# Preactivation convolution: half sums multiplied an image ahead and written by the vector engine to where the convolution accumulates; three of eight images combined

## The chip, the cores and the metric

The kernel runs on one core of a Trainium2 chip. The metric is the device time of one launch in microseconds (us), the median of several runs. The core has five engines that run their own instruction queues in order: TensorE (PE, with its weight loads shown as PEld), VectorE (DVE), ScalarE (ACT), GpSimd (POOL) and SyncE (SP). They wait for one another by semaphores. Matmuls accumulate in PSUM; everything else lies in SBUF.

## The reference

160 images of 128 channels and 32x32 pixels. Each is group-normalised (32 groups of 4 channels), convolved 3x3 with padding 1 by one of five weight sets (image i of the input uses set i mod 5), and added to the unnormalised input. The weights are quantised from U with two step sizes taken from the range of all of U.

```python
s1 = (beta - alpha) / 3.0                       # beta, alpha: max and min of U
v1 = s1 * floor(U / s1)
s2 = s1 / 5.0
v2 = s2 * floor((U - v1) / s2)
w = (v1 + v2).reshape(OUT_CH * N, IN_CH, K, K)
...
xb = x.reshape(B // N, N * C, H, W)
act = conv_general_dilated(xb, w, window_strides=(1, 1), padding=[(1, 1), (1, 1)], feature_group_count=N)
...
m = jnp.mean(g, axis=(2, 3, 4), keepdims=True)  # g: (B, 32, 4, 32, 32)
s = jnp.var(g, axis=(2, 3, 4), keepdims=True)
gn = ((g - m) / jnp.sqrt(s + eps)).reshape(v.shape)
...
x = x + conv(gn(x), U)
```

## The kernel before, in words

The kernel takes the images set by set: image i of the program (0 to 159) belongs to set i // 32. In SBUF an image is a tile of 128 partitions (channels) by 1024 pixels. A matmul takes one 128x128 weight tap and up to 512 pixels, so an image's output, called eo, fills two PSUM banks of 16 rows each.

The normalised image is used as a sum of two fp16 parts, high and low. For an ordinary image the high part is convolved directly (`taps`, L590): three columns of taps, each 3 rows of taps by 2 banks, 18 matmuls. The low part is convolved through pairs of rows: with d (differences of rows two apart) and s, t (sum and difference of the two rows of a pair), the tap rows g0, g1, g2 give an even and an odd output row as d times g0 or -g2, plus half of (m1 + m2) or (m1 - m2), where m1 = s times (g0 + g1 + g2) and m2 = t times (g0 - g1 + g2). So there are 6 wide matmuls for m1, m2 (PSUM tile m, two banks) and 12 of half width for d. A combined image (`combined`, L504; before: every third one from image 14 to 155) treats both parts this way: 12 wide and 24 half-width matmuls, and no direct taps. `combine` (L514) forms d, s and t in fp32 from the raw image, `high_combined` (ACT) rounds it to fp16, `low_combined` (DVE) takes the rest.

The loop of `run` (from L845) has one iteration for each image. The order of every engine's queue is written out by hand: what `run` calls first comes first on that engine. In iteration i of the kernel before:

- PE: `conv(i)`: m1 and m2 of image i (first, or after the first column of taps if image i-1 is combined), and its taps or products into eo. Two small statistics matmuls (`means`, `variances`) come between columns, once for each group of eight images.
- ACT: for image i+14 the two passes of the statistics (`image_sum` L193, `image_square` L200), `leave(i)` (L674), which copies m1 and m2 from PSUM to SBUF, then `normalise` and `high_part` (L493, L501) of image i+3, or `high_combined` (L537) of image i+2.
- DVE: `low_combined` (L543) or `low_part` (L550), `residual(i-1)` (L707, L709: eo plus the half sums into an fp32 tile sum), `combinations` (L563 to L566), one or two of the 14 steps for a column of the next set's weights (`make_column`), and `pairs(i)` (L686, L687), which forms m1 + m2 and m1 - m2 in SBUF.
- POOL: `accumulate` (L722) issues a DMA that adds sum to the image in SBUF; the small vectors of the statistics (L220 to L245) and two edge rows of `combine` (L522, L523) are computed here.
- SP: issues loads 20 images ahead and stores two images behind.

[...]eo has two buffers of two banks (pool `ps_eo`), m one buffer of two banks (`ps_m`), the statistics one bank and the weight transposes one. Images 0 to 2 are convolved directly in both parts, and the last four are added and stored by hand (`by_hand`). Statistics of images 8, 10, 12 and 14 are made on DVE by bn_stats (L183), all others from image 8 on by ACT.

## Time and profile before

| What | us |
|---|---|
| median of the runs | 1043.59 (1042.65 to 1043.96) |
| the profiled execution, its own time | 1041.9 |
| its span in the profile | 1040.1 |
| PE busy | 995.6 |
| DVE busy | 937.8 |
| ACT busy | 848.7 |
| POOL busy | 436.4 |

The span is the time from the first to the last instruction that the profiler recorded; the execution's own time lies 1.8 us above it. Busy time is the sum of the stretches in which the engine had an instruction. A line number such as L709 is a line of the kernel; a group of instructions shows its count, its busy time, the mean duration of one, and what ended the engine's idle time ahead of it. DVE and ACT start an instruction slightly before the recorded end of the one ahead, so an instruction takes up less of its queue than its recorded duration. The granted TensorE clock was 0.993 of full speed as a mean.

### The profile page before, as it was taken

How to read it: one execution, taken by the hardware profiler on the slowest of the kernel's cores; microseconds unless marked ns; L12 is line 12 of the kernel's file. 1: busy time of each engine (PE TensorE's matmuls, PEld its weight loads, DVE VectorE, ACT ScalarE, POOL GpSimd, SP SyncE). 2: the span in 40 equal slices, each digit the busy share in tenths (PEclk: the TensorE clock that was granted, in tenths of full speed). 3: DMA queues.
4: the chain of work that ended last, by engine and by line, in shares of the span. 5: the costliest groups of instructions: out<-in, count | busy, mean ns of one | idle time of the engine just before them, and what ended most of it. 6: DMA issues, size and time to landing. Idle time of an engine off the chain costs nothing. (4 is left out here: it accounts for less than half of the span.)

```text
span 1040.1 us, 15860 instructions
## 1 busy us (share of the span) xinstructions
PE 995.6 (96%) x5910; PEld 578.5 (56%) x5910; DVE 937.8 (90%) x1374; ACT 848.7 (82%) x1133; POOL 436.4 (42%) x494
## 2 busy tenths in 40 slices
PE   1899998999999999999999999999989999999997
PEld 0455565565655556565555555655545556555553
DVE  8998798998999999889999989998979898888885
ACT  4899796998888888888888889888869988886551
POOL 4432435361454566253545362634554523334210
PEclk9999999999999999999999999999989999999999
DMA  9559988899999889999999999999988999988673
GB/s 370 211 152 233 252 236 229 215 269 273 284 271 255 240 237 264 265 281 256 253 252 268 250 255 258 276 273 266 225 236 222 271 284 241 264 205 220 163 182 125
DMA packets 67286, 254.42 MB, mean 245 GB/s; under 512 B 5248, under 2 KB 5248, under 8 KB 67200
## 3 DMA queue, kind: packets, MB, share of 16 engines
q1 hardware_dynamic: 45168, 173.09, 48.6%
q0 software_dynamic: 22032, 80.23, 40.3%
q8 instruction: 48, 0.79, 0.3%
q14 instruction: 38, 0.31, 0.1%
HBM read 89.19 MB, written 83.89 MB: 166 GB/s over the span
## 5 line engine op out<-in xcount | busy, mean ns | idle before, releaser
L590 PE MATMUL eo<-hi,wt 128*128 128x496 f16 (+3 forms) x1998 | 481.4, 378 | 2.5 <-DVE sum L709 1.2
L626 PEld LDWEIGHTS <-wt 128*128 128x128 f16 x3690 | 361.7, 98 | 217.5 <-issue 2.4
L722 POOL DMA_DIRECT2D xt<-sum x153 | 135.6, 888 | 488.0 <-DVE sum L709 319.1
L590 PEld LDWEIGHTS <-wt 128*128 128x128 f16 x2070 | 203.7, 100 | 196.4 <-issue 6.5
L626 PE MATMUL eo<-rows,wt 128*128 128x248 f16 (+1 forms) x1308 | 197.4, 274 | 0.0
L200 ACT ACTIVATE junk<-xt,mv 128x1024 f16<-128x1024 f32 x156 | 178.6, 1145 | 1.7
L193 ACT ACTIVATE junk<-xt 128x1024 f16<-128x1024 f32 x156 | 164.4, 1054 | 11.7 <-DMA xt<-in_x_dram 10.1
L626 PE MATMUL m<-rows,wt 128*128 128x496 f16 (+1 forms) x654 | 159.2, 380 | 0.0
L674 ACT ACTIVATE mm<-m 128x1024 f16<-128x1024 f32 x109 | 111.0, 1018 | 58.2 <-PE m L626 55.9
L543 DVE SCALAR_TENSOR_TENSOR vl<-v,rstd,vh 128x2048 f16<-128x2048 f32 x48 | 112.7, 2347 | 45.7 <-ACT vh L537 45.7
L493 ACT ACTIVATE z<-xt,shift,rstd 128x1024 f32<-128x1024 f32 x112 | 138.0, 1232 | 6.1 <-POOL shift L243 6.1
L550 DVE TENSOR_TENSOR lo<-z,hi 128x1024 f16<-128x1024 f32 x112 | 137.1, 1224 | 6.4 <-ACT hi L501 6.4
L709 DVE SCALAR_TENSOR_TENSOR sum<-pq,eo 128x1024 f32<-128x1024 f16 x105 | 127.1, 1210 | 3.4 <-PE eo L626 3.4
L501 ACT CAST hi<-z 128x1024 f16<-128x1024 f32 x112 | 116.1, 1036 | 0.4
L537 ACT ACTIVATE vh<-v,rstd 128x2048 f16<-128x2048 f32 x48 | 95.8, 1997 | 23.5 <-POOL v L523 23.0
L626 PE MATMUL eo<-vl,wt 128*128 128x248 f16 (+1 forms) x576 | 110.1, 273 | 0.0
L626 PE MATMUL eo<-vh,wt 128*128 128x248 f16 (+1 forms) x576 | 110.1, 273 | 0.0
L626 PE MATMUL m<-vh,wt 128*128 128x496 f16 (+1 forms) x288 | 110.1, 382 | 0.0
L626 PE MATMUL m<-vl,wt 128*128 128x496 f16 (+1 forms) x288 | 109.9, 382 | 0.0
L674 ACT ACTIVATE mw<-m 128x1024 f32<-128x1024 f32 x48 | 49.1, 1023 | 60.5 <-PE m L626 60.3
L522 POOL TENSOR_SCALAR v<-xt,ngm 128x32 f32<-128x32 f32 x48 | 90.6, 1888 | 0.0
L563 DVE TENSOR_TENSOR rows<-lo 128x1024 f16<-128x1024 f16 x109 | 74.2, 681 | 0.1
(113 smaller groups left out, 971.0 us busy)
## 6 DMA issues: line engine op xcount, KB each, us to landing
xt<-in_x_dram SPq DMA_DIRECT2D x78, 1024.0 KB, 9.2
out_dram<-xt SPq DMA_DIRECT2D x78, 1024.0 KB, 5.3
xt<-sum POOLq DMA_DIRECT2D x153, 512.0 KB, 6.8
range<-in_L_conv_U_dram SPq DMA_DIRECT2D x4, 576.0 KB, 6.4
u<-in_L_conv_U_dram SPq DMA_DIRECT2D x4, 576.0 KB, 12.0
xt<-in_x_dram SPq DMA_DIRECT2D x4, 512.0 KB, 9.4
out_dram<-xt SPq DMA_DIRECT2D x3, 512.0 KB, 2.8
u<-in_L_conv_U_dram SPq DMA_DIRECT2D x2, 288.0 KB, 3.0
```

Source lines behind the costliest of these rows:

```text
L193: self.nc.scalar.activation(junk, image, ACTF.Copy, scale=-1.0 / image.shape[1], accum_out=self.mv[:, j, 0:1],)
L200: self.nc.scalar.activation(junk, image, ACTF.Square, bias=self.mv[:, j, 0:1], accum_out=self.mv[:, j, 1:2],)
L493: nc.scalar.activation(z, self.image(i), ACTF.Identity, bias=st.shift[:, j : j + 1], scale=st.rstd[:, j : j + 1],)
L501: self.nc.scalar.copy(hi.rearrange("p h w -> p (h w)"), self.z[i])
L537: self.nc.scalar.mul(vh, self.v[i], st.rstd[:, j])
L543: self.nc.vector.scalar_tensor_tensor(vl, self.v[i], st.rstd[:, j], self.hi[i], ALU.mult, ALU.subtract)
L550: self.nc.vector.tensor_sub(lo[:, 1 : self.H + 1, :].rearrange("p h w -> p (h w)"), self.z.pop(i), self.hi[i].rearrange("p h w -> p (h w)"),)
L590: nc.tensor.matmul(target[:, h, r0 - h0 : r1 - h0, c0:c1], self.wts[n, col][:, k, :], tile[:, s0 : s0 + r1 - r0, c0 + dw : c1 + dw], start ...
L626: nc.tensor.matmul(target[:, :, c0:c1], self.wts[n, col][:, kind, :], source[:, :, c0 + dw : c1 + dw], start=start, stop=stop,)
L674: self.nc.scalar.mul(m, self.m.pop(i).rearrange("p a i w -> p a (i w)"), scale)
L709: nc.vector.scalar_tensor_tensor(self.sum[i], self.m.pop(i), 0.5 / UP, eo, ALU.mult, ALU.add)
L722: self.nc.gpsimd.dma_start(self.image(i), self.sum.pop(i), accum_op=ALU.add)
```

## The change

The multiplications that form m1 and m2 move an image ahead: iteration i now begins on PE with `sums_of_pairs(i + 1)`, ahead of the taps of image i. ACT copies only m2 to SBUF (`leave(i + 1)`, 512 elements in place of 1024). DVE adds and subtracts m1, read from PSUM, and m2, and writes the two results straight into the PSUM banks of eo of image i+1 (`pairs(i + 1)`). The matmuls of that image then accumulate on what lies there: no matmul of an image from 3 on has `start=True` in eo. Since eo then holds twice the result, the direct taps and the taps for d are kept doubled, and the factor 0.5 is applied as the result leaves PSUM: `residual` becomes one ScalarE instruction (for the last four images it stays on DVE). The fp16 copies of the half sums and their scale UP go.

Combined images are now those with i mod 8 in (1, 4, 6), 53 of them in place of 48. Statistics of images with i mod 8 in (1, 5), from image 9 on, are made by DVE. The order within an iteration is rewritten, `combine` comes two iterations earlier, the buffers of vh go from one to two and those of sum from three to four, and the transposes of a weight column go into the next iteration.

The diff, without blank lines and cut to its core:

```diff
     STEADY = 14
+    COMBINED = (1, 4, 6)
+    MEASURED = (1, 5)
     EARLY = 8
...
         self.wide = pool("wide", 1)
-        self.wide_parts = pool("wide_parts", 1)
+        self.wide_parts = pool("wide_parts", 2)
         self.evac = pool("evac", 2)
-        self.sums = pool("sums", 3)
+        self.sums = pool("sums", 4)
...
+            self.keep_column(n, col, self.turn_column(n, col, parts))
         else:
             m = self.qpool.tile([P, P, ROW], MM, tag="m", name=f"m{n}_{col}")
-            yield nc.vector.scalar_tensor_tensor(m, k1, 5.0, k2, ALU.mult, ALU.add)
-            parts = ((m, self.ident),)
+            nc.vector.scalar_tensor_tensor(m, k1, 5.0, k2, ALU.mult, ALU.add)
+            self.columns.append((n, col, ((m, self.ident),)))
+            yield
...
+        return pt
+    def keep_column(self, n, col, pt):
+        nc, P = self.nc, self.P
         wt = self.wpool.tile([P, 6, P], MM, tag=f"wt{col}", name=f"wt{n}_{col}")
-        nc.scalar.mul(wt[:, self.G, :], pt, 1.0 / LIFT)
-        nc.scalar.mul(wt[:, self.MINUS_G2, :], pt[:, 2, :], -1.0 / LIFT)
+        half = self.qpool.tile([P, ROW, P], MM, tag="half", name=f"half{n}_{col}")
         outer = self.qpool.tile([P, P], MM, tag="outer", name=f"outer{n}_{col}")
-        nc.gpsimd.tensor_tensor(outer, wt[:, 0, :], wt[:, 2, :], ALU.add)
-        nc.gpsimd.tensor_tensor(wt[:, self.SUM, :], outer, wt[:, 1, :], ALU.add)
-        nc.gpsimd.tensor_tensor(wt[:, self.DIFF, :], outer, wt[:, 1, :], ALU.subtract)
+        nc.scalar.mul(wt[:, self.G, :], pt, 2.0 / LIFT)
+        nc.scalar.mul(half, pt, 1.0 / LIFT)
+        nc.gpsimd.tensor_tensor(outer, half[:, 0, :], half[:, 2, :], ALU.add)
+        nc.gpsimd.tensor_tensor(wt[:, self.SUM, :], outer, half[:, 1, :], ALU.add)
+        nc.gpsimd.tensor_tensor(wt[:, self.DIFF, :], outer, half[:, 1, :], ALU.subtract)
+        nc.gpsimd.tensor_scalar_mul(wt[:, self.MINUS_G2, :], wt[:, 2, :], -1.0)
         self.wts[n, col] = wt
...
     def by_vector(self, i):
-        return self.EARLY <= i < self.EARLY + 8 and i % 2 == 0
+        return i >= self.EARLY and i % 8 in self.MEASURED
     def measure(self, i, stages=(0, 1)):
@@ -503,7 +521,7 @@
     def combined(self, i):
-        return self.STEADY <= i < self.imgs - LAST and i % 3 == 2
+        return self.STEADY <= i < self.imgs - LAST and i % 8 in self.COMBINED
     def column_of(self, i):
...
                     tile[:, s0 : s0 + r1 - r0, c0 + dw : c1 + dw],
-                    start=(col == self.COLS[0] and k == 1 and top == 0),
+                    start=(i < self.FIRST and col == self.COLS[0] and k == 1 and top == 0),
                     stop=(last and k == 2),
+                    skip_group_check=True,
                 )
...
+    def product(self, target, i, kind, source, col, start, stop):
+        n, _ = self.place(i)
+        dw = col - 1
+        c0, c1 = max(0, -dw), self.W - max(0, dw)
+        self.nc.tensor.matmul(
+            target[:, :, c0:c1],
+            self.wts[n, col][:, kind, :],
+            source[:, :, c0 + dw : c1 + dw],
+            start=start,
+            stop=stop,
+            skip_group_check=True,
+        )
...
+    def both(self, i):
+        return [self.halves(v) for v in ([self.hi[i]] if self.combined(i) else []) + [self.v[i]]]
+    def sums_of_pairs(self, i):
+        m = self.m[i] = self.banks(self.ps_m, "m", i)
+        both = self.both(i)
+        for a, kind in enumerate((self.SUM, self.DIFF)):
+            for col in self.COLS:
+                for j, (_, st) in enumerate(both):
+                    self.product(
+                        m[:, a], i, kind, st[:, a], col,
+                        col == self.COLS[0] and j == 0,
+                        col == self.COLS[-1] and j == len(both) - 1,
+                    )
     def conv(self, i, on_the_way):
-        nc, W = self.nc, self.W
-        n, _ = self.place(i)
-        combined = self.combined(i)
-        if combined:
-            both = [self.halves(v) for v in (self.hi[i], self.v.pop(i))]
-        else:
-            both = [self.v.pop(i)]
-        late = self.combined(i - 1)
...
-        if not late:
-            sums_of_pairs()
-        eo = self.eo[i] = self.banks(self.ps_eo, "eo", i)
+        if i + 1 < self.imgs:
+            self.sums_of_pairs(i + 1)
+        eo = self.eo[i]
         for col in self.COLS:
-            if col == self.COLS[1] and late:
-                sums_of_pairs()
             if col != self.COLS[0]:
                 on_the_way(col)
-            if not combined:
+            last = col == self.COLS[-1]
+            if not self.combined(i):
                 self.taps(i, (self.hi[i], 0), col, eo, False)
             for a, kind in enumerate((0, self.MINUS_G2)):
-                for d, _ in both:
+                both = self.both(i)
+                for j, (d, _) in enumerate(both):
                     for h in range(2):
                         rows = slice(h * 16 + a, h * 16 + 16, 2)
-                        to = eo[:, h].rearrange("p (i a) w -> p i a w", a=2)[:, :, a, :]
-                        product(
-                            to, kind, d[:, rows, :], col,
-                            combined and col == self.COLS[0] and a == 0 and d is both[0][0],
-                            col == self.COLS[-1] and a == 1 and d is both[-1][0],
+                        to = eo[:, h].rearrange("p (i a) w -> p a i w", a=2)[:, a]
+                        self.product(
+                            to, i, kind, d[:, rows, :], col, False,
+                            last and a == 1 and j == len(both) - 1,
                         )
+        del self.v[i]
     def leave(self, i):
...
-        if self.combined(i):
-            m = self.wide.tile([self.P, 2, 512], F32, tag="m", name=f"mw{i}")
-            scale = 0.5
-        else:
-            m = self.evac.tile([self.P, 2, 512], MM, tag="mm", name=f"mm{i}")
-            scale = UP
-        self.nc.scalar.mul(m, self.m.pop(i).rearrange("p a i w -> p a (i w)"), scale)
-        self.m[i] = m
+        m2 = self.evac.tile([self.P, self.H // 2, self.W], F32, tag="m2", name=f"m2_{i}")
+        self.nc.scalar.copy(m2, self.m[i][:, 1])
+        self.m[i] = self.m[i], m2
...
     def pairs(self, i):
         nc = self.nc
-        m = self.m.pop(i).rearrange("p a (i w) -> p a i w", w=self.W)
-        if self.combined(i):
-            pq = self.wide.tile([self.P, 1024], F32, tag="pq", name=f"pqw{i}")
-        else:
-            pq = self.evac.tile([self.P, 1024], MM, tag="pq", name=f"pq{i}")
-        rows = pq.rearrange("p (i a w) -> p i a w", a=2, w=self.W)
-        nc.vector.tensor_add(rows[:, :, 0], m[:, 0], m[:, 1])
-        nc.vector.tensor_sub(rows[:, :, 1], m[:, 0], m[:, 1])
-        self.m[i] = pq
-        if self.by_hand(i):
-            xj = self.image(i)
-            nc.vector.scalar_tensor_tensor(xj, pq, 0.5 / UP, xj, ALU.mult, ALU.add)
+        m, m2 = self.m.pop(i)
+        eo = self.eo[i] = self.banks(self.ps_eo, "eo", i)
+        rows = eo.rearrange("p h (i a) w -> p (h i) a w", a=2)
+        nc.vector.tensor_add(rows[:, :, 0], m[:, 0], m2)
+        nc.vector.tensor_sub(rows[:, :, 1], m[:, 0], m2)
...
         if not self.by_hand(i):
             self.sum[i] = self.sums.tile([self.P, 1024], F32, tag="sum", name=f"sum{i}")
-            if self.combined(i):
-                nc.vector.tensor_add(self.sum[i], eo, self.m.pop(i))
-                return
-            nc.vector.scalar_tensor_tensor(
-                self.sum[i], self.m.pop(i), 0.5 / UP, eo, ALU.mult, ALU.add
-            )
+            nc.scalar.mul(self.sum[i], eo, 0.5)
             return
         xj = self.image(i)
         halves = [slice(0, 512), slice(512, 1024)] if i == self.imgs - 1 else [slice(0, 1024)]
         for h in halves:
-            nc.vector.tensor_add(xj[:, h], eo[:, h], xj[:, h])
+            nc.vector.scalar_tensor_tensor(
+                xj[:, h], eo[:, h], 0.5, xj[:, h], ALU.mult, ALU.add
+            )
...
-        ready, middle, measured, loaded, later = [], [], self.EARLY, 6, None
+        ready, middle, measured, loaded = [], [], self.EARLY, 6
+        later, turned = iter(()), []
...
                     for st in ready:
                         st.means()
+                    for *column, parts in self.columns:
+                        turned.append((column, self.turn_column(*column, parts)))
+                    self.columns.clear()
...
             if i < self.FIRST:
+                if i == self.FIRST - 1:
+                    self.sums_of_pairs(self.FIRST)
                 j = (i - 1) % self.FIRST
                 self.direct_hi(j, self.COLS[2])
@@ -863,79 +871,70 @@
...
-                self.residual(j)
                 for col in self.COLS:
                     on_the_way(col)
             else:
+                j = i - 1
                 self.conv(i, on_the_way)
             ahead = i + min(10 + i // 2, self.STAT_LEAD + 1)
             to_measure = range(measured, min(self.imgs, ahead))
             measured += len(to_measure)
...
-            parted = [
-                k for k in (i + 3, i + 4)
-                if self.FIRST < k < self.imgs and not self.combined(k)
-                and k - 3 - (self.combined(k - 1) and self.group_of[k] == self.group_of[k - 1])
-                == i
-            ]
-            if b == self.per_set // 16 and n + 1 < N_SETS:
-                self.load_set(n + 1)
-            if b == self.per_set // 8 and n + 1 < N_SETS:
-                later = (s for col in self.COLS for s in self.make_column(n + 1, col))
+            if n + 1 < N_SETS:
+                if b == (2 if n == 0 else 0):
+                    self.load_set(n + 1)
+                if b == (4 if n == 0 else 2):
+                    later = (s for col in self.COLS for s in self.make_column(n + 1, col))
             by_scalar = [k for k in to_measure if not self.by_vector(k)]
...
+            if i != self.FIRST:
+                self.residual(j)
+                self.accumulate(j)
+            if self.combined(i + 1):
+                for k in by_scalar:
+                    self.measure(k, (0,))
+            if self.FIRST <= i + 1 < self.imgs:
+                self.leave(i + 1)
+            if not self.combined(i + 1):
+                for k in by_scalar:
+                    self.measure(k, (0,))
+            part = self.FIRST < i + 3 < self.imgs
+            if self.combined(i + 3):
+                self.high_combined(i + 3)
+            elif part:
+                self.normalise(i + 3)
             for k in by_scalar:
-                self.measure(k, (0,))
-            if self.combined(i - 1):
-                for k in by_scalar:
-                    self.measure(k, (1,))
-            if i >= self.FIRST and not self.combined(i):
-                self.leave(i)
-            for k in parted:
-                self.normalise(k)
-            if self.combined(i):
-                self.leave(i)
-            elif not self.combined(i - 1):
-                for k in by_scalar:
-                    self.measure(k, (1,))
-            for k in parted:
-                self.high_part(k)
-            low = i + 2 if self.FIRST < i + 2 < self.imgs and not self.combined(i + 2) else None
-            if self.combined(i + 1):
-                self.low_combined(i + 1)
-            if self.combined(i + 2):
-                self.combine(i + 2)
-                self.high_combined(i + 2)
-            if low is not None:
-                self.low_part(low)
-            if i > self.FIRST:
-                self.residual(i - 1)
-                self.accumulate(i - 1)
-            if low is not None:
-                self.combinations(low)
-            if later is not None:
-                take(later, 1)
-            if i >= self.FIRST:
-                self.pairs(i)
-            if later is not None:
-                take(later, 1)
-                if b == self.per_set - 1:
-                    run(later)
+                self.measure(k, (1,))
+            if part and not self.combined(i + 3):
+                self.high_part(i + 3)
             for st in middle:
                 st.deviation()
                 st.scales()
             for st in ready:
                 st.deviations()
+            for column, pt in turned:
+                self.keep_column(*column, pt)
+            turned = []
+            low = i + 2 if self.FIRST < i + 2 < self.imgs and not self.combined(i + 2) else None
+            if self.combined(i + 2):
+                self.low_combined(i + 2)
+            if low is not None:
+                self.low_part(low)
+            take(later, 1)
+            if low is not None:
+                self.combinations(low)
+            if self.FIRST <= i + 1 < self.imgs:
+                self.pairs(i + 1)
+            if self.combined(i + 4):
+                self.combine(i + 4)
+            else:
+                take(later, 1)
+            if b == self.per_set - 4:
+                run(later)
             middle, ready = ready, []
-            if self.combined(i):
-                for k in by_scalar:
-                    self.measure(k, (1,))
             for k in to_measure:
                 if self.by_vector(k):
                     self.measure(k)
```

## The prediction

> **What bounds the kernel now.** I read the page's busy shares first, then the chain that ended last, in a window of steady state, then PE's waits from 55 us on.
>
> ```profile
> PE 995.6 (96%) x5910; PEld 578.5 (56%) x5910; DVE 937.8 (90%) x1374; ACT 848.7 (82%) x1133; POOL 436.4 (42%) x494
> ```
> ```profile
> 820.97 2.59 PE m L626 x12
> 823.56 2.63 PE eo L626 x24
> 826.19 1.27 PE eo L590 x6
> ...
> 832.61 1.30 PE m L626 x6
> ...
> 839.03 2.59 PE m L626 x12
> ```
>
> The chain (start, length, work) is PE without a gap. A combined image takes 2.59 + 2.63 = 5.22 us. The ordinary one behind it runs from 826.19 to 832.61: 6.42 us, of which 1.29 are m and 5.13 the taps and d. Three images take 18.06 us, PE is the bound, and DVE (90%) is not far behind.
>
> ```profile
> PE pg L226 <- POOL dv L223: 10.2, 6, 3.2
> PE eo L590 <- DVE sum L709: 1.2, 2, 1.0
> ```
>
> These are all of PE's waits after the start: six times `variances` waited for POOL, 10.2 us in all. Behind the two longest (2.95 and 3.21 us, at 166 and 761 us) the granted clock falls: the windows by stretch show 0.86 and 0.85 over 162 to 174 us, 0.53 and 0.79 over 760 to 770 us. That is 0.14 x 6 + 0.15 x 6 + 0.47 x 5 + 0.21 x 5 = 5.1 us more.
>
> The durations come from the groups by form (count, busy us, mean ns):
>
> ```profile
> L709 DVE SCALAR_TENSOR_TENSOR sum<-pq,eo 128x1024 f32<-128x1024 f16 x105 | 127.1, 1210 | 3.4 <-PE eo L626 3.4
> L716 DVE TENSOR_TENSOR xt<-eo,xt 128x512 f32<-128x512 f32 x2 | 1.3, 686 | 2.0 <-PE eo L626 2.0
> L686 DVE TENSOR_TENSOR pqw<-mw 128x512 f32<-128x512 f32 x48 | 33.2, 692 | 10.3 <-ACT mw L674 10.3
> L674 ACT ACTIVATE mw<-m 128x1024 f32<-128x1024 f32 x48 | 49.1, 1023 | 60.5 <-PE m L626 60.3
> L458 ACT ACTIVATE wt<-pt 128x384 f16<-128x384 f32 x15 | 7.2, 483 | 7.3 <-PE pt L453 7.3
> L550 DVE TENSOR_TENSOR lo<-z,hi 128x1024 f16<-128x1024 f32 x112 | 137.1, 1224 | 6.4 <-ACT hi L501 6.4
> ```
>
> What a queue pays is the time from start to next start, which the ordered listing gives (us): low part 1.14, combinations 0.60 + 0.34 + 0.34 = 1.28, `combine` on DVE 1.07 + 0.66 + 0.61 = 2.34, L686 fp32 0.61; on ACT L193 1.10 and L200 1.22 with their accumulator reads, z 1.14, hi 0.94, L674 0.92. From PE's last slot to ACT's start pass 0.20 us (502.30 to 502.50), from DVE's end to PE 0.06 (727.78 to 727.84).
>
> [...]
>
> **The change, part by part.** PE: an ordinary image keeps 6.42 us, a combined one 5.22. 53 - 48 = 5 more combined images: 5 x 1.20 = **-6.0 us**. The order m(i+1), then image i, moves work but adds none.
>
> ACT: leave falls from 1024 to 512 elements. From 384 and 1024 elements out of PSUM (483 and 1018 ns) the slope is 0.836 ns, so 0.59 us, 0.49 in the queue. `residual` adds 153 x 1.02 = +156 us, leave gives back 67, and 34 images whose statistics go to DVE give back 34 x 2.58 = 88 (two passes of 1.054 and 1.145, two reads of 0.19). Combined images and weight columns: +2. ACT stays at about 850.
>
> DVE: residual -185 (127.1 + 58.2); pairs from 157 (fp16 0.416, fp32 0.69 each) to 157 x 2 x 0.69 = 217; additions by hand -5; bn_stats 34 x 1.87 = +64; five more combined images 5 x (4.93 - 2.74) = +11. Sum about 883, 55 less.
>
> POOL has five more pairs of edge rows and one small instruction per weight column: below 20 us in an engine idle for 58% of the span. Its `accumulate` is issued earlier; loads and stores stay in SP's order. More buffers and the moved transposes (0.17 us each on PE, as now) I cost at nothing.
>
> The new wait decides. At the start of iteration i PE waits for `pairs(i)`, since it frees m's only buffer and fills eo. Everything on PE is queued behind it. `pairs(i)` needs `leave(i)`, which sits in ACT's queue behind the work of iteration i-2 and behind `residual(i-2)`; and it sits in DVE's queue behind `low_part` and `combinations` of image i+1, which wait for hi of that image, late in ACT's iteration. PE's iterations are now uneven: from 7.72 us (ordinary, next combined) to 3.92 (2.63 + 1.29: combined, next ordinary). I laid the three queues out over eight images. Every `pairs` is in time but one. Counted from PE's start of an iteration with i mod 8 = 4, the chain is:
>
> ACT: m 1.29, to ACT 0.20, leave 0.49, first pass 1.10, z 1.14, second pass 1.22, hi 0.94, visible after 0.10: 6.48. DVE: low part 1.14, weight step 0.30, combinations 1.28, pairs of image 6 1.22: 10.42. Then `combine` 2.34, low part 1.14, step 0.30, combinations 1.28, pairs of image 7 1.30, to PE 0.06: **16.84 us**. PE's own work up to there is 3.92 + 7.72 + 3.92 = **15.56**. The stall is 1.28 us in each period. The 0.30 is an average: 12 columns x 14 steps over 142 images, 0.50 each, two places per image. Without steps the stall is 0.68, with both 1.68. From image 20 to 148 there are 17 such periods: **+21.8 us**.
>
> The writes to PSUM are unknown: no DVE instruction here has PSUM as destination. The nearest row is 686 ns. Below, 0.60 us[...] makes the stall 0.92 and the sum 15.6; above, 0.85 us[...] makes it 1.94 and 33. I take 0.69.
>
> The wait also comes at the start: `pairs(3)` follows hi(4) (ACT's queue puts its end near 57.9 us), low part, combinations and itself, to 61.6; PE is through with the direct images at 57.2. A stall of 4.5 us, with a slow clock after it such as above (some 2): **+6.5**.
>
> The waits on POOL: ngm of a group leaves ACT 1.7 us into iteration 3, its four dv instructions take 1.46 + 0.61 + 0.39 + 0.35 = 2.8, and PE comes to `variances` 6.0 us into it. That slack of 1.5[...] should take most of 16.5 us (waits 11.4, clock 5.1): **-12**.
>
> Sum: -6.0 - 12 + 6.5 + 21.8 = +10.3. The profiled execution took 1041.9 (span 1040.1 and 1.8 around it), the median is 1.7 above: 1043.6 + 10.3 = 1053.9. Since stalls also absorb some other waits, I say **1052 us**, with 1044 to 1061 as its own range.
>
> **Rivals.** (1) Faster: the queues keep up. Every term of the chain would be slightly shorter (shorter waits, PSUM writes near 0.5 us), so the 1.28 vanishes. For: the margins are small, DVE's total falls by 55 us[...]. Against: the chain adds measured durations. It gives 1043.6 - 6.0 - 12 + 6.5 = 1032; up to a stall of (6.0 + 12 - 6.5)/17 = 0.68 us, a chain of 16.24, the kernel is not slower. (2) Slower still: writes to PSUM cost 0.85 us or more, or the edge rows of `combine` (POOL, behind the statistics) hold up vh on ACT. Other iterations then stall too, since pairs(5) has a margin of 0.15 us, pairs(2) 0.5: a period grows to 50 or 51 us from 49.0 (47.76 of PE work plus 1.28), that is 1062 to 1080. (3) No difference: gain and stalls cancel, as at a chain of 16.24; 1042 to 1046. (4) The values in PSUM are overwritten by the first matmul: the output changes but not the time, so it needs no chance of its own.
>
> **How the numbers follow.** A measurement of this kernel can tell about 0.2% (2.1 us) from no change. Likeliest case 0.52 (nearly all slower), rival 1 0.22, rival 2 0.15, rival 3 0.11. Faster 0.22, same 0.11, slower 0.67. The range leaves out half of rival 1 and a third of rival 2: 1033 to 1070.
>
> **What would show it.** Right: PE's waits for DVE at `pairs`, about 17 of 1 to 2 us at i mod 8 = 7, near 20 us in all, and one of 4 to 5 us near 57 us; `variances` hardly waits; a two-step `pairs` of 0.69 us each; DVE near 883, ACT near 850; a period of 49 to 50 us over eight images. Wrong: a period near 48 us with PE unbroken (rival 1), or PE's waits in several iterations of the period and `pairs` above 0.8 us (rival 2). The start is wrong if PE doesn't pause before image 3.

## The result, and the profile after

| What | before (us) | after (us) |
|---|---|---|
| median of the runs | 1043.78 (1042.65 to 1047.85) | 1061.26 (1055.82 to 1062.9) |
| the profiled execution, its own time | 1041.9 | 1055.82 |
| its span | 1040.1 | 1054.1 |
| mean granted TensorE clock in it | 0.993 | 0.995 |

The ratio of the times, after to before, is 1.0149 with a 95% interval of 1.0109 to 1.0188: slower by 1.5%. The forecast was 1052 with a range of 1033 to 1070.

The busy shares of the page after:

```profile
PE 990.0 (94%) x5910; PEld 574.7 (55%) x5910; DVE 909.0 (86%) x1387; ACT 845.4 (80%) x1145; POOL 363.4 (34%) x519
```

Every engine has less busy time than before (PE 5.6 us, DVE 29, ACT 3, POOL 73), and the span is 14 us longer. So the time is not in work but in waiting. PE's waits (waiting instruction, what it waited for, us in total, times, longest):

```profile
PE m L634 <- DVE eo L697: 28.7, 21, 5.2
PE rows L435 <- DVE ext L427: 18.3, 1, 18.3
PE pg L225 <- POOL dv L222: 7.1, 3, 4.7
```

The first line of waits is the new one: the first matmul into m waits for the second instruction of `pairs`. The longest of the 21, 5.2 us, comes before image 3; 23.5 us are left, of which 16 waits of 0.86 to 2.22 us make 22.4. All 16 stand at i mod 8 = 7. The second line is the wait for the range of U at the start, 16.9 us in before's profile; the other ten profiles, one of them of the kernel before with another choice of combined images, have 17.6 to 19.1, so the 1.4 us more are not put down to the change. The third was 17.0 us before; of the 10.2 us of it after 55 us nothing is left.

Here is the chain in one of these periods, from PE's start of an iteration with i mod 8 = 4 (start, length, work):

```profile
526.60 1.31 PE m L634 x6
...
527.94 0.02 ACT m L687
...
528.42 1.15 ACT junk L192 x2
529.57 1.13 ACT z L511
...
531.83 0.94 ACT hi L519
...
532.80 1.23 DVE lo L568
534.02 0.47 DVE lt L111
...
537.13 1.06 DVE v L544
...
539.45 1.14 DVE lo L568
540.59 0.27 DVE k L112
...
542.77 0.71 DVE eo L697
...
543.53 1.47 PE m L634 x6
```

Three engines hand the work on. ACT must do a pass of the statistics (L192), `normalise` (L511) and the second pass before it makes hi; DVE's queue stops at `low_part` until then, and only behind it come the `pairs` of two images and a `combine` (L544). The new operations themselves, by form (count, busy us, mean ns, idle before and its cause):

```profile
L696 DVE TENSOR_TENSOR eo<-m,m 128x512 f32<-128x512 f32 x157 | 108.9, 693 | 29.0 <-ACT m L687 27.0
L697 DVE TENSOR_TENSOR eo<-m,m 128x512 f32<-128x512 f32 x157 | 109.8, 700 | 5.4
...
L711 ACT ACTIVATE sum<-eo 128x1024 f32<-128x1024 f32 x153 | 156.2, 1021 | 97.1 <-PE eo L634 88.4 <-DVE mv L186 8.5
L568 DVE TENSOR_TENSOR lo<-z,hi 128x1024 f16<-128x1024 f32 x107 | 130.9, 1224 | 55.3 <-ACT hi L519 55.3
```

None is slow: writing to PSUM takes 693 and 700 ns, and `leave` (L687) 584. The last line is the one to look at: DVE idled 55.3 us in front of `low_part`, waiting for hi. Before it was 6.4 us.

To see where the 14 us lie, I cut both traces at PE's start of image 23 and of image 143. After the change, m of the next image is multiplied first, so before's marks are set 1.29 us later (the m of an ordinary image) to stand at about the same amount of work. Image 23, and likewise 143, is combined before and ordinary after, so the first and the last row are uncertain by about as much; the middle row is not.

| Stretch | before (us) | after (us) | difference |
|---|---|---|---|
| to image 23 (after: with the stall in front of it) | 187.99 + 1.29 = 189.3 | 194.6 | +5.3 |
| images 23 to 142 | 929.72 - 187.99 = 741.7 | 943.48 - 194.59 = 748.9 | +7.2 |
| the rest | 1040.1 - 931.0 = 109.1 | 1054.1 - 943.5 = 110.6 | +1.5 |

The first row contains the 1.4 us of the wait for the range of U.

### The profile page after: what moved, and what is told of

It is laid out like the page before. It is cut to its first block, busy times and chain, and to the rows that moved or that the text cites. A ratio compares the mean times of both kernels' runs of the same rounds, so it can differ in the third digit from the quotient of the medians.

```text
span 1054.1 us, 15898 instructions
## 1 busy us (share of the span) xinstructions
PE 990.0 (94%) x5910; PEld 574.7 (55%) x5910; DVE 909.0 (86%) x1387; ACT 845.4 (80%) x1145; POOL 363.4 (34%) x519
## 4 chain that ended last, share of the span: by engine, by line
PE 69%; DVE 21%; ACT 6%; issue 3%; DMA 1%; POOL 0%; SPq 0%; DVEq 0%; ACTq 0%
PE eo L608 32%; PE m L634 20%; PE eo L634 15%; DVE lo L568 4%; DVE eo L697 2%; DVE rows L582 2%; DVE eo L696 2%; ACT junk L192 2%; ACT z L511 2%; DVE v L544 2%; ACT hi L519 1%; DVE rows L584 1%; DVE rows L585 1%; DVE v L547 1%; DVE v L550 1%
## 5 line engine op out<-in xcount | busy, mean ns | idle before, releaser
L608 PE MATMUL eo<-hi,wt 128*128 128x496 f16 (+1 forms) x1908 | 458.7, 377 | 1.1 <-ACT wt L476 1.1
L608 PEld LDWEIGHTS <-wt 128*128 128x128 f16 x1980 | 194.6, 100 | 186.5 <-issue 4.2
L711 ACT ACTIVATE sum<-eo 128x1024 f32<-128x1024 f32 x153 | 156.2, 1021 | 97.1 <-PE eo L634 88.4
L568 DVE TENSOR_TENSOR lo<-z,hi 128x1024 f16<-128x1024 f32 x107 | 130.9, 1224 | 55.3 <-ACT hi L519 55.3
L561 DVE SCALAR_TENSOR_TENSOR vl<-v,rstd,vh 128x2048 f16<-128x2048 f32 x53 | 124.4, 2347 | 22.8 <-ACT vh L555 22.8
L199 ACT ACTIVATE junk<-xt,mv 128x1024 f16<-128x1024 f32 x122 | 139.2, 1141 | 0.3
L192 ACT ACTIVATE junk<-xt 128x1024 f16<-128x1024 f32 x122 | 129.4, 1061 | 11.5 <-DMA xt<-in_x_dram 11.3
L696 DVE TENSOR_TENSOR eo<-m,m 128x512 f32<-128x512 f32 x157 | 108.9, 693 | 29.0 <-ACT m L687 27.0
L511 ACT ACTIVATE z<-xt,shift,rstd 128x1024 f32<-128x1024 f32 x107 | 132.9, 1242 | 0.6 <-POOL shift L242 0.6
L687 ACT COPY m<-m 128x512 f32<-128x512 f32 x157 | 91.6, 584 | 49.6 <-PE m L634 49.6
L634 PE MATMUL eo<-vh,wt 128*128 128x248 f16 (+1 forms) x636 | 121.7, 273 | 0.0
L634 PE MATMUL eo<-vl,wt 128*128 128x248 f16 (+1 forms) x636 | 121.7, 273 | 0.0
L634 PE MATMUL m<-vl,wt 128*128 128x496 f16 (+1 forms) x318 | 120.7, 380 | 0.0
L697 DVE TENSOR_TENSOR eo<-m,m 128x512 f32<-128x512 f32 x157 | 109.8, 700 | 5.4
## 6 DMA issues: line engine op xcount, KB each, us to landing
xt<-in_x_dram SPq DMA_DIRECT2D x4, 512.0 KB, 10.3
```

The lines of the kernel that those rows point to most:

```text
L192: self.nc.scalar.activation(junk, image, ACTF.Copy, scale=-1.0 / image.shape[1], accum_out=self.mv[:, j, 0:1],)
L199: self.nc.scalar.activation(junk, image, ACTF.Square, bias=self.mv[:, j, 0:1], accum_out=self.mv[:, j, 1:2],)
L511: nc.scalar.activation(z, self.image(i), ACTF.Identity, bias=st.shift[:, j : j + 1], scale=st.rstd[:, j : j + 1],)
L561: self.nc.vector.scalar_tensor_tensor(vl, self.v[i], st.rstd[:, j], self.hi[i], ALU.mult, ALU.subtract)
L568: self.nc.vector.tensor_sub(lo[:, 1 : self.H + 1, :].rearrange("p h w -> p (h w)"), self.z.pop(i), self.hi[i].rearrange("p h w -> p (h w)"),)
L608: nc.tensor.matmul(target[:, h, r0 - h0 : r1 - h0, c0:c1], self.wts[n, col][:, k, :], tile[:, s0 : s0 + r1 - r0, c0 + dw : c1 + dw], start ...
```

## The experiments

The theory under test: the loss is the stall at i mod 8 = 7, which is set by ACT's queue in iteration 4 (through hi) and not by the cost of the new operations, the totals, or the choice of combined images. The main rivals: that some total of work is too large, that the start is the larger part, and that combining three of eight is to blame. The kernel before was run again beside each batch (medians 1042.99, 1043.92 and 1043.36 us), and every ratio below is to those runs.

### Another image's statistics to DVE

```diff
-    MEASURED = (1, 5)
+    MEASURED = (2, 5)
```

Statistics run 14 images ahead, so an image with i mod 8 = 2 is measured in an iteration with i mod 8 = 4. This takes both passes out of ACT's queue there and puts two into iteration 3. Number and kind of the instructions stay.

> One constant of the changed kernel: DVE takes the statistics of images with i mod 8 in (2, 5) in place of (1, 5); the amount of work on each engine stays. My theory: the recurring stall comes from one chain that starts in iteration 4 of eight (two ACT passes, z, hi, then DVE's low part, combinations, pairs, combine and again to pairs of image 7: 16.84 us against 15.56 of PE work). The two passes of iteration 4 leave ACT (2.32 us) and go to DVE where it waits for hi anyway, so the stall vanishes: PE's waits for pairs fall from 28.7 us to about 6 (the start), the time to 1036 to 1041 us. Rival (pairs on DVE behind leave on ACT is too slow for PE's short iterations whatever ACT does ahead of it, or DVE's total is what binds): nothing moves by more than 5 us, 1055 to 1062.

Measured: 1040.11 us (1038.62 to 1041.8), ratio to before 0.9976 (0.9969 to 0.9983). The page and PE's waits:

```profile
PE 986.8 (95%) x5910; PEld 575.1 (55%) x5910; DVE 909.6 (88%) x1387; ACT 847.6 (82%) x1145; POOL 365.3 (35%) x519
```
```profile
PE m L634 <- DVE eo L697: 15.5, 12, 5.2
```

DVE, ACT and POOL have the same busy time as in the changed kernel, within 2.2 us, and 21 us are gone. Between the two profiled executions, 16.6 us apart, PE's waits at `pairs` fell by 13.2 us and its busy time by 3.2; the rest of the 21 is that the changed kernel's profiled execution was the fastest of its five. I had expected the stall to vanish, with some 6 us of waits in all. What is left apart from the start are waits of 0.79 to 1.35 us in periods in which weight columns are made (and one of 0.23), and none after 783 us, where no column is. The edit moves two ACT passes and the bn_stats of an image, and no amount of work; where they stand decides the sign of the result.

### The same passes, behind the high part

Here the statistics stay on ACT, but where i mod 8 is 4 or 5 both passes come after hi:

```diff
+            behind = by_scalar if i >= self.STEADY and i % 8 in (4, 5) else []
+            by_scalar = [k for k in by_scalar if k not in behind]
...
             if part and not self.combined(i + 3):
                 self.high_part(i + 3)
+            for k in behind:
+                self.measure(k)
```

> The changed kernel with another cut through the same chain: in iterations with i mod 8 in (4, 5), from image 14 on, ACT does both statistics passes behind high_part in place of around normalise. No engine's work changes, only ACT's order. My theory: hi of images 7 and 8 comes 2.3 us sooner, the chain falls below PE's 15.56 us and the stall goes: 1037 to 1042 us, PE's waits for pairs near 6 us. Rival (DVE's total or the short iterations bind): 1055 to 1062 as before.

Measured: 1039.63 us (1037.64 to 1041.35), ratio 0.9965 (0.9956 to 0.9973). PE's wait at `pairs`:

```profile
PE m L634 <- DVE eo L697: 12.7, 14, 5.2
```

Now not even the queue's contents change, only the order within two of eight iterations. With 5.2 us at the start, 7.5 us of waits are left of 23.5, where I had expected about 1.

### Behind the high part in one iteration only

The same edit with `i % 8 in (4,)`.

> As the second experiment, but with the two passes behind high_part only in iterations with i mod 8 = 4. hi of image 7 comes 2.3 us sooner, but ACT as a whole finishes iteration 4 no sooner, so hi of image 8 in iteration 5 does not, and low part 8, combinations and pairs of image 7 wait for it: a chain of 16.4 us takes the place of 16.84. Theory: only 0.2 to 0.5 us per period come back, 1052 to 1058 us. Rival (the lateness of hi of image 7 alone makes the stall): 1038 to 1042 as in the second experiment.

Measured: 1055.34 us (1052.8 to 1057.21), ratio 1.0118 (1.0091 to 1.0145). PE's wait at `pairs` is as it was:

```profile
PE m L634 <- DVE eo L697: 28.8, 21, 5.2
```

So hi of iteration 4 is not alone: the stall is nearly as long (1.12 and 1.03 us at 494 and 544 us against 1.09 and 1.20). The number came as expected, but the chain is not the one I expected, by way of hi of image 8. Two of DVE's groups, which in the changed kernel idled 29.0 and 55.3 us (shown above):

```profile
L696 DVE TENSOR_TENSOR eo<-m,m 128x512 f32<-128x512 f32 x157 | 108.9, 694 | 60.8 <-ACT m L687 59.2
L568 DVE TENSOR_TENSOR lo<-z,hi 128x1024 f16<-128x1024 f32 x107 | 131.5, 1229 | 25.7 <-ACT hi L519 25.5
```

The wait moved from `low_part` (L568) to `pairs` (L696). In each of the 16 periods DVE now idles 1.3 to 2.9 us ahead of `pairs` of image 6, until `leave` of that image (L687). In ACT's queue the two passes that went behind hi stand ahead of that `leave`, with a `residual` and the first statistics pass of iteration 5. Ahead of the `low_part` of image 8 DVE does not wait at all. The first chain in my prediction was right, but a second one lay directly under it: the prediction names `leave` as a condition of `pairs`, but writes down no chain through it. The median is 5.9 us lower although the waits are as before; the granted clocks are higher (0.994 to 0.997 against 0.988 to 0.995), and why is not shown.

### One place worse

```diff
-    MEASURED = (1, 5)
+    MEASURED = (3, 5)
```

The two passes now stay in iterations 3 and 4 and leave iteration 5. The totals are again the same.

> The opposite of the first experiment by the same constant: DVE takes the statistics of images with i mod 8 in (3, 5). Image i+14 with 3 mod 8 falls into iteration 5, where DVE is inside the chain; iteration 3 gets two ACT passes instead. Theory of the chain: 1.55 us of bn_stats are added to DVE's part between pairs of images 6 and 7, so the stall grows from 1.3 to about 2.8 us per period of eight images, 17 x 1.55 = 26 us: 1081 to 1090 us. Rival (DVE's total binds): the total is the same, 1055 to 1062.

Measured: 1098.63 us (1097.3 to 1107.71), ratio 1.0534 (1.0512 to 1.0557). PE's waits, the page's busy line, and windows around one pause (stretch, length, busy time and instructions of PE, PEld, DVE, ACT and POOL, granted clock, share of DMA, GB/s):

```profile
PE m L634 <- DVE eo L697: 55.1, 17, 7.0
```
```profile
PE 1009.5 (91%) x5910; PEld 580.6 (52%) x5910; DVE 910.8 (82%) x1387; ACT 847.9 (77%) x1145; POOL 351.7 (32%) x519
```
```profile
625.00:628.00 3.00, 0.00 (x0) 0.00 (x0) 2.97 (x7) 2.34 (x4) 0.36 (x1) 1.00 1.02 318
628.00:631.00 3.00, 2.80 (x10) 1.21 (x11) 3.00 (x4) 1.22 (x2) 0.49 (x1) 0.75 1.08 229
631.00:634.00 3.00, 3.00 (x13) 1.44 (x12) 2.97 (x6) 1.54 (x2) 0.00 (x0) 0.69 1.03 259
```

This profiled execution, the longest of five at 1107.71 us, lies 51.9 us above the profiled one of the changed kernel. The waits at `pairs` grew by 26.4 us, two new ones for `residual` (L711) add 5.9, and PE's busy time rose by 19.5 for the same 5910 matmuls: 51.8 in all. The last of the three is TensorE's own speed: behind a pause of 3.8 us ending at 628.2 the granted clock was 0.75 and 0.69 for six microseconds, and 1.00 again from 634 us on. The stalls at `pairs` grew as forecast, and where forecast: bn_stats stands between `combine` and `low_part` on DVE, and in the changed kernel's trace such a block takes up 1.69 us (574.11 to 575.80). My 1081 to 1090 held neither of the other two.

### Every third image combined, as before

```diff
-        return self.STEADY <= i < self.imgs - LAST and i % 8 in self.COMBINED
+        return self.STEADY <= i < self.imgs - LAST and i % 3 == 2
```

> The changed kernel with the old choice of combined images, every third one; the image-ahead order and the write into PSUM stay. PE has 6.0 us more work. Laid out in the same way, the period of three would leave a stall of 1.4 us per eight images, much as with three of eight. Theory: 1061 to 1068 us. Rival (the unevenness of three of eight makes the stalls): with the stalls gone 1040 to 1046 us.

Measured: 1065.68 us (1063.73 to 1068.09), ratio 1.0227 (1.0204 to 1.0249); `pairs` keeps PE waiting for 27.2 us in 19 places. The pattern of combined images is not the cause: the stalls stay without it. Without the five more combined images the kernel is 4.4 us slower still, where 6.0 us of PE work were at stake.

### The kernel before, with three of eight combined

The opposite half of the change: in the kernel before, `combined` takes the images with i mod 8 in (1, 4, 6).

```diff
-        return self.STEADY <= i < self.imgs - LAST and i % 3 == 2
+        return self.STEADY <= i < self.imgs - LAST and i % 8 in (1, 4, 6)
```

> The kernel before with one part of the change alone: combined images are those with i mod 8 in (1, 4, 6), everything else, order and half sums too, as before. My sum says 6.0 us less PE work: 1036 to 1039 us if the old order copes. Rival: images 4 and 6 are two apart and share one buffer v, DVE has five more combined images to make and is 96% loaded where weights are made, so PE waits and the gain is lost: 1044 to 1060 us.

Measured: 1059.17 us (1057.37 to 1061.26), ratio 1.0159 (1.0137 to 1.0181). PE's waits:

```profile
PE pg L226 <- POOL dv L223: 26.6, 14, 4.7
...
PE m L626 <- ACT mm L674: 8.1, 3, 2.7
```

Six microseconds of PE work that the sum saves turn into 16 us lost: PE's busy time falls by only 0.8 us, to 994.8, `variances` waits for POOL 26.6 us in place of 17.0, m waits for ACT, and DVE has 952.1 us of work in place of 937.8. Why POOL is so much later is not isolated; that a pattern of eight falls in step with the statistics' groups of eight is a guess. The 6 us that I gave to this part of the change are there only together with the other parts, as the run with every third image suggests. The image-ahead order and the write into PSUM were not tried one without the other.

### The start

`sums_of_pairs(3)` goes behind the direct taps of iteration 1, with its `leave` and `pairs` there:

```diff
             if i < self.FIRST:
-                if i == self.FIRST - 1:
-                    self.sums_of_pairs(self.FIRST)
...
+                if i == self.FIRST - 2:
+                    self.sums_of_pairs(self.FIRST)
...
+            if i == self.FIRST - 2:
+                self.leave(self.FIRST)
+                self.pairs(self.FIRST)
```

> The changed kernel with m of image 3, its leave and its pairs moved from iteration 2 to iteration 1, so that PE need not wait before image 3. My theory: the single stall of 5.2 us at 59 us goes, and with it the slow clock behind it (some 2 us): 5 to 7 us less, 1053 to 1056 us. Rival: ACT is the bound of the first images, so what PE gains at once it loses before image 14: less than 2 us.

Measured: 1060.5 us (1053.84 to 1061.17), ratio 1.017 (1.0153 to 1.0187). The span of the profiled execution is 1052.1 us against 1054.1 for the changed kernel; the medians differ by 0.8. PE's two waits for DVE:

```profile
PE m L634 <- DVE eo L697: 23.4, 20, 2.2
PE m L634 <- DVE rows L584: 3.7, 1, 3.7
```

The wait of 5.2 us for `pairs(3)` is gone and one of 3.7 us stands there for `combinations(4)`, the other operand of the same matmuls. I had expected 5 to 7 us; the rival had the size (less than 2 us) and the kind, that what PE gains at once it loses again, here at the next matmuls. In the changed kernel `pairs(3)` stands behind `low_part(4)` in DVE's queue, and `combinations(4)` needs its result, so it was the whole head of the loop that was late, and not one hand-off.

### Four of eight

```diff
-    COMBINED = (1, 4, 6)
-    MEASURED = (1, 5)
+    COMBINED = (0, 2, 4, 6)
+    MEASURED = (2, 6)
```

> The changed kernel with every second image combined, i mod 8 in (0, 2, 4, 6), and DVE taking the statistics of (2, 6). PE's work falls by 18 x 1.20 = 21 us against three of eight (71 combined images in place of 53). A combined image costs DVE 4.6 us in place of 2.4, so DVE nears 95% where weights are made. Theory: long and short iterations of PE alternate, so that every late pairs falls into a long one; no stall without weight steps, up to 0.8 us per eight images with them: 1018 to 1030 us. Rival (DVE or the edge rows on POOL bind): 1040 us or more.

Measured: 1043.37 us (1042.14 to 1044.78), ratio 0.9997 (0.9988 to 1.0006). PE's busy time falls to 975.0 us, but it waits at `pairs` in 45 places, 31.9 us in all. DVE has 942.4 us of work (90%), and waits 18.9 us for hi, 17.1 us for m2 and 16.2 us for vh; ACT waits 27.3 us for the edge rows of POOL. PE's gain is eaten by many small waits. I had expected 1018 to 1030; the rival's 1040 or more is what came.

### Further in the good direction

The order of the second experiment in more iterations: i mod 8 in (2, 4, 5), and in all eight.

> The changed kernel with both ACT passes behind high_part in the iterations with i mod 8 in (2, 4, 5), from image 14 on. With two weight steps per iteration my layout of the queues leaves 0.2 us of stall per eight images, where (4, 5) alone leaves 0.45. Theory: 2 to 4 us less than the second experiment, 1035 to 1038 us. Rival (the statistics come late and hold up means, or the remaining waits are elsewhere): 1039 or more.

> As the run before it, with the passes behind high_part in all iterations from image 14 on; in iterations ahead of a combined image too, where the changed kernel puts the first pass ahead of leave. The layout gives the same 0.2 us per eight images: 1035 to 1038 us. Rival: the last image of a group is measured just ahead of its means matmul, so PE now waits for ACT once in eight images: 1040 or more.

Measured: 1038.85 us (1038.11 to 1039.44), ratio 0.9955 (0.9938 to 0.9971), for the first, and 1040.04 us (1039.48 to 1041.7), ratio 0.9972 (0.9961 to 0.9984), for the second. PE waits at `pairs` for 12.9 us in the one and 14.2 us in the other, 5.2 of each at the start. Both miss the expected 1035 to 1038. The second has the rival's number, but not its reason: no wait of `means` for ACT shows in the steady state.

The first has the lowest median of all: 22 us below the changed kernel and 4.5 below the kernel before. Its interval overlaps that of the two-iteration order, so it is not shown to be better than that one. Moving the passes in all eight iterations brought nothing more.

## Why the prediction was right

**The mechanism.** "PE's waits for DVE at `pairs`, about 17 of 1 to 2 us at i mod 8 = 7, near 20 us in all, and one of 4 to 5 us near 57 us": there were 16, at that place, 22.4 us in all, and one of 5.2 us ending at 64.6 us. The period was 49.9 us on average, where 49 to 50 was forecast. The seventeenth period that the forecast counted, with its stall before image 151, is the exception that fits: in iteration 148 there is no image left to take statistics of (148 + 14 lies behind the last), ACT's queue is shorter, and PE does not wait. The first two experiments show that the stall hangs on where the statistics stand in ACT's queue: move two passes and 21 us are gone. The third shows that they must be out of the way of `leave` as well as of hi. Rival 1 (no stall) and rival 2 (dear writes to PSUM, stalls in many iterations) fall with the same trace: `pairs` took 0.69 and 0.70 us where 0.69 was forecast.

**The size.** The rise was forecast as 8.4 us and came as 17.5. The median lies 0.3 us above the 1044 to 1061 that I gave to the likeliest case by itself. It lies inside the forecast only because the range went up to 1070 for the sake of rival 2, and rival 2 did not come. So the place and the kind of the loss were foreseen, and the number was within the range in part by luck. One number of the forecast doesn't follow from its own terms: rival 2's periods of 50 or 51 us, 17 of them, give 1070 to 1087 us, not 1062 to 1080. And the 0.60 and 0.85 us for a write to PSUM were assumptions of mine, which no trace showed. The likeliest case used none of these.

**The chain.** From PE's start of iteration 4 at 526.44 (in the ordered listing) to its start at 543.53 it took 17.09 us, where the sum gave 16.84. Its terms:

| Term | forecast (us) | measured (us) |
|---|---|---|
| to hi, seen by DVE | 6.48 | 6.36 |
| low part, step, combinations, pairs of image 6 | 3.94 | 4.33 |
| `combine` | 2.34 | 2.32 |
| low part to pairs of image 7, and to PE | 4.08 | 4.08 |

The 0.39 in the second row are a weight step of 0.47 in place of the average 0.30, and about 0.1 each for the low part (1.22 us to the next piece of the listing, where it had waited for hi, against 1.14 for the later one) and for `pairs` (1.34 in place of 1.22). PE's last slot before the stall ended at 542.17, so that PE's own work took 15.73, of which 0.16 is a small wait for m in iteration 5: 15.57, where 15.56 was forecast. The recorded wait of 1.20 us is counted from the recorded end of the last two matmuls, 542.33, which is 0.16 us behind their slot: such a pair has 0.38 us in the record, and the next pair starts 0.22 us behind its start. From slot to start this stall costs PE 1.36 us, and the wait list shows 0.16 us less.

**The other terms.** PE work -6.0: its busy time fell by 5.6, though both busy times contain some microseconds of slow clock, so that this is no exact confirmation. POOL's waits -12: all 10.2 us of them after 55 us went, and POOL's first edge row (L522, L540 after) fell from 1888 ns to 793:

```profile
L522 POOL TENSOR_SCALAR v<-xt,ngm 128x32 f32<-128x32 f32 x48 | 90.6, 1888 | 0.0
```
```profile
L540 POOL TENSOR_SCALAR v<-xt,ngm 128x32 f32<-128x32 f32 x53 | 42.1, 793 | 0.0
```

The start +6.5: the wait is 5.2 us, and behind it the windows give a clock of 0.59 over 64 to 67 us and 0.84 over 67 to 70, so 0.41 x 3 + 0.16 x 3 = 1.7 us, together 6.9. The size was right. Two things were left out of its working: on DVE `residual(1)`, which waits for PE's direct taps, stands ahead of `low_part(4)`; and PE is through with the direct images at 59.4 us in place of 57.2. Of these 2.2 us, 1.4 are the wait for the range of U, which differs as much from run to run.

**The steady stretch.** For images 23 to 142 the forecast's own terms are: 45 combined images in place of 40, -6.0; before's waits in that stretch, 9.8 + 1.2 - 2.95 = 8.05 us (the one at 166 us lies ahead of it), and 3.4 us of slow clock at 760 us, -11.5; 15 stalls of 1.28 us, +19.2. That makes +1.7, and +7.2 was measured. The stalls' recorded waits are 20.1 us, three small ones add 0.9, and 15 times the 0.16 us between slot and recorded end makes 23.4. With a slow clock of 1.7 us behind one of them (below), that is 5.9 us more than forecast: it closes the difference, to half a microsecond.

**The terms that were mis-sized.** So the stalls were put too low by some 4 us in all, by these 0.16 us each and by weight steps that cost more than their average (0.47 us in place of 0.30 in the chain above). The larger term seems to be the clock. I wrote "stalls also absorb some other waits" and took the sum of +10.3 down to 1052; and I took the 5 us of slow clock behind before's pauses as regained. The profiled execution came out 13.9 us above before's, and the median 17.5. The five executions of the changed kernel, the profiled one being the fastest, show what goes with the higher median (which is of four of them, without 1059.13):

| time (us) | 1055.82 | 1059.13 | 1060.41 | 1062.11 | 1062.9 |
|---|---|---|---|---|---|
| mean granted clock | 0.995 | 0.992 | 0.991 | 0.988 | 0.989 |

A clock lower by 0.006 over 1060 us is 6.4 us, and that is about the distance of the last from the first. The new pauses bring a slow clock of their own. In windows of the changed kernel around two equal pauses (columns as above), of 2.04 us ending at 594.07 and 2.09 us ending at 793.91:

```profile
594.00:597.00 3.00, 2.93 (x16) 1.51 (x17) 3.00 (x4) 2.53 (x5) 0.85 (x1) 1.00 1.01 325
```
```profile
793.00:796.00 3.00, 2.09 (x8) 0.94 (x9) 2.96 (x4) 2.25 (x4) 0.81 (x1) 0.83 1.06 261
796.00:799.00 3.00, 3.00 (x12) 1.35 (x10) 2.96 (x6) 2.42 (x3) 0.05 (x1) 0.60 1.07 213
```

Behind the first the clock stays at 1.00; behind the second it falls, which costs 0.17 x 3 + 0.40 x 3 = 1.7 us. The 0.83 and 0.60 are means over 3 us: in windows of 1 us the clock is 1.00 up to 795 us, 0.50 from there to 798, 0.79 to 799 and 1.00 again. What chooses between the pauses stays open, since no experiment here isolated it. That the medians of the changed kernel and of the one with its statistics one place worse are raised in this way is a reading of clock and time side by side, strong in the latter (0.981 to 0.983 in four executions, 0.973 in the one at 1107.71 us), not an experiment by itself.

**DVE's total.** Forecast 883, measured 909.0. The sum over DVE's groups fell from 1035.1 to 985.6, by 49.5 where 55 was forecast. The busy time fell by less, 28.8, since it counts overlapping records once, and the overlap fell from 97.3 to 76.6 us. That DVE's waits break up the back-to-back runs is the likely reason; nothing in the result hung on it.

## What to carry to other kernels

Before moving a hand-off a step ahead, lay out each in-order queue over the whole period of the pattern and follow the first consumer back, instruction by instruction: here totals that were all lower gave a slower kernel, and one constant that moves the statistics of an image from one place to another was worth -21 us or +37. When one link is shortened, write down the next chain under it too, since the stall can stay where it was, as it did here, and look in the trace for which chain it is: the time came as expected while the link was another. Price a pause on TensorE above its recorded length: here by the 0.16 us between the last slot and its recorded end, and by 1.7 us of slow clock behind one pause of 2.09 us, where one of 2.04 us had none.

## What the runs showed of the hardware

- Writing 512 fp32 elements per partition to PSUM from DVE (693 and 700 ns, one operand from PSUM) took the same time as writing them to SBUF did (692 and 687 ns, both operands from SBUF).
- The granted TensorE clock fell to 0.50 for some 3 us behind a pause of 2.09 us, beginning 1.1 us after work had started again, and stayed at 1.00 behind one of 2.04 us in the same execution. Where pauses of 2.6 to 3.9 us came in each period, PE's busy time for the same matmuls grew by 19.5 us.
- POOL's first edge row (L522, L540 after) took 793 ns in place of 1888 as a mean, without a change of its own, and another POOL instruction went the other way (L240, L239 after, from 752 to 1675 ns). The cause is not shown: the order of the queues and several of DVE's instructions changed together.
